# A four-layer graph network on one core: quarter sums, plane splits and merged additions change engines, and the planner's durations change

## The chip, the cores and the metric

The kernel runs on one core of a Trainium2 chip. The metric is the device time of one launch in microseconds (us), lower is better. A core has five engines with queues of their own: TensorE (PE, with its weight loads as PEld), VectorE (DVE), ScalarE (ACT), GpSimd (POOL) and SyncE (SP), which here only issues DMAs. Each queue runs in the order in which it was written. TensorE writes into eight banks of PSUM (512 fp32 values per partition each), and VectorE and ScalarE bring the results from there to SBUF.

## What is computed

The input is 128 graphs of 64 nodes with 512 features, and one 64 x 64 adjacency matrix for all. Four layers follow each other, all in fp32:

```python
h = relu(layernorm(x))
x = x + attention0(h)          # q, k, v with bias, 8 heads of 64, masked softmax
h = relu(layernorm(x))
x = x + attention1(h) @ Wo + bo
h = relu(layernorm(x))
x = x + normalised((h Wq)(h Wk)^T * adj) @ (h Wv)      # no softmax, rows divided by their norm
h = relu(layernorm(x))
o = attention3(h) @ w_proj + b_proj
x = x + o + layernorm(o) * gamma + beta
```

## The kernel before

**Tiling.** The 8192 rows are cut into 16 blocks of 512 rows, eight graphs each. The main loop runs over n = 0 to 63, 16 blocks for each of the four layers. In layers 0, 1 and 3 an iteration does the projections q, k and v of its block, the scores, and the values product of the block before; layers 1 and 3 add an output projection o, one or two iterations later. Layer 2 has two projections (`a2`, in which two weights are folded into one, and `v2`).

**Projections.** A projection is a 512 x 512 x 512 product. It is not done with eight block products of 256 but with seven, in the manner of Strassen and Winograd: sums of blocks of the input (`S`, or `SO` for the output projection; made by `sums_x`), sums of blocks of the weights (made once per weight), and additions of the seven products into the four blocks of the result. A part of the seven is split again in the same way into products of 128: the table `LEVEL2` says which, "423" for most. For such parts `sums_q` makes four more sums of 128 columns from the input's blocks, and the products of 128 are added in quarters. In `projection`, the string `parts` is "423" or "43", products "a", "b" and "c" are those whose quarters go to several blocks, and `add(dst, ps)` adds a PSUM bank to the result on VectorE. For the first product of a block `copy` or `copy_4` brings the bank over on ScalarE (with the bias of q and k), and products that are needed twice go to the small tiles `p5`, from which GpSimd adds them.

**Layer norm and transposes.** For a block, VectorE takes mean and variance, GpSimd the inverse root, ScalarE normalises (`xin`). The projections want the block with features on the partitions. `turn` does this by DMA: the fp32 values are split into two planes of 16 bits (tile `z`, 1024 elements of uint16), a DMA transposes them (`hp`), and ScalarE weaves them together into `hT`. The splitting copy is an argument with the default `dve.tensor_copy`; for the softmax weights the call hands over `act.copy`.

**Which engine makes the sums.** `sums_x` takes an engine for the block sums, and for the quarter sums of each part it chooses VectorE if the part is in `ON_DVE` (which is "2"), else GpSimd:

```python
        for q in parts:
            on = dve if q in ON_DVE else gps
            x[q] = sums_q(x[int(q)], room, (eng if eng is dve else on).tensor_tensor, fine and q != "3")
```

**The order of the work.** The code does not issue instructions. It records them in a `Plan`, which orders them and then issues all in `issue`, for which reason every instruction stands under one line of the profile, L285 (in the changed kernel this line has the number 291). `Plan.order` is a list scheduler: each step has a busy time and a lateness from `duration`, it becomes ready when its inputs are, and of the ready steps the planner takes the one that can start first, and of equals that with the lowest rank. The rank is the time at which the work must be done for TensorE to run in the recorded order, plus an offset per kind of step from the table `PREFER`. Steps that read PSUM get `HASTE` taken off the rank. The planner also gives out the eight banks. A block of PSUM is opened by its first product and its bank is free when its last reader is done. `PORT` is a lateness that also marks VectorE instructions with two inputs in SBUF, which the planner lets exclude GpSimd. Thus a new duration or offset can move any instruction on any queue, DMA issues included.

**Names in the profile.** `mm` is any of the PSUM banks; `w` any weights; `kT`, `qT`, `v` results of projections (`kT` also holds the result of o in layer 3); `oT` the attention's output, `SO` its sums; `s` the scores; `xo` the block to which the layer's result is added; `p` the tiles `p5`.

Of the kernel before, what the change touches and what calls it, by code (L numbers as in the profile page):

```python
# [56 lines left out]
class Plan:  # L57
# [106 lines left out]
    def order(self):  # L164
# [56 lines left out]
        opened, first = set(), 0  # L221
        self.start, self.bank = {}, {}
        while len(self.start) < n:
            best = None
            idle = sorted(t for b, t in enumerate(freed) if b not in holds)
            for e in engines:
                pick = None
                for i in here[e]:
                    at = max(ready[i], free[e])
# [34 lines left out]
            for h in uses[i]:  # L264
                last[h] = max(last.get(h, 0.0), at + busy + (0.0 if e == "tensor" else late))
                left[h] -= 1
                if not left[h]:
                    del holds[self.bank[h]]
                    freed[self.bank[h]] = last[h]
            for u, lag in users[i]:  # L270
                same = self.steps[u][0] == e
                ready[u] = max(ready[u], at + busy - lag + (0.0 if same and not moves else late))
                wait[u] -= 1
                if not wait[u]:
                    here[self.steps[u][0]].append(u)
# [35 lines left out]
class Pool:  # L311
# [28 lines left out]
PORT = 150.5  # L340
# [5 lines left out]
ON_DVE = "2"  # L346
WINDOW = 6
RESERVE = 0
HASTE = 0.0
PREFER = {  # L350
    "gps dma_start out_0_dram<-xo 2048": -12683,
    "gps dma_start x1<-kT": -7145,
    "gps dma_start x1<-row": -3460,
    "gps dma_start x1<-xo": -18648,
    "gps memset mhalf<- 8": 4917,
    "gps memset ones<- 1": -3867,
    "gps tensor_scalar ve<-mv 1": 622,
    "gps tensor_scalar ve<-mv 4": -1287,
    "gps tensor_tensor S2<-S 128": 9247,
    "gps tensor_tensor S2<-S2 128": -37406,  # L360
    "gps tensor_tensor S<-S 512": -89087,
    "gps tensor_tensor S<-hT 512": -1496,
    "gps tensor_tensor SO2<-SO 128": 12636,
    "gps tensor_tensor SO2<-SO2 128": 10398,
    "gps tensor_tensor SO<-oT 512": 2203,
    "gps tensor_tensor hT<-hT 128": 1226,
    "gps tensor_tensor kT<-kT 128": 5636,
    "gps tensor_tensor kT<-kT 256": 3369,
    "gps tensor_tensor kT<-kT 512": -42897,
    "gps tensor_tensor oT<-oT 128": 2476,  # L370
    "gps tensor_tensor qT<-qT 128": -134,
    "gps tensor_tensor qT<-qT 256": -1241,
    "gps tensor_tensor rn<-ss 8": -17140,
    "gps tensor_tensor row<-hT 128": -1603,
    "gps tensor_tensor row<-row 128": 8443,
    "gps tensor_tensor rs<-ve 1": 12875,
    "gps tensor_tensor s<-hT 128": -26189,
    "gps tensor_tensor s<-s 1024": -13182,
    "gps tensor_tensor s<-s 128": -40765,
    "gps tensor_tensor v<-v 128": -615,  # L380
    "gps tensor_tensor w<-w 128": -892,
    "gps tensor_tensor w<-w 512": 3785,
    "gps tensor_tensor xo<-xo 128": 44131,
    "gps tensor_tensor xo<-xo 512": -445,
    "sca activation kT<-mm 128": -119261,
    "sca activation kT<-mm 256": -39612,
    "sca activation qT<-mm 128": -41982,
    "sca activation qT<-mm 256": -11513,
    "sca activation s<-s 1024": 49040,
    "sca activation s<-s 256": 11077,  # L390
    "sca activation xin<-xin 512": 38622,
    "sca copy hT<-hp 1024": 66109,
    "sca copy hT<-mm 512": 10088,
    "sca copy kT<-mm 128": -16208,
    "sca copy kT<-mm 512": -19133,
    "sca copy oT<-mm 512": -12905,
    "sca copy p5<-mm 128": 237,
    "sca copy qT<-mm 128": 625,
    "sca copy qT<-mm 256": 54924,
    "sca copy qT<-mm 512": 3166,  # L400
    "sca copy s<-hp 1024": 447,
    "sca copy s<-mm 512": 10472,
    "sca copy v<-mm 128": 7235,
    "sca copy v<-mm 256": -3409,
    "sca copy v<-mm 512": -11450,
    "sca copy w<-mm 128": -19703,
    "sca copy w<-mm 256": -8441,
    "sca copy xo<-mm 128": 3488,
    "sca copy xo<-mm 256": -4935,
    "sca copy z<-mm 512": 4852,  # L410
    "sca copy z<-s 1024": 11870,
    "syn dma_start SO<-in_L2_gnn_Wk_dram": -11583,
    "syn dma_start a2d<-z": 2446,
    "syn dma_start adj2<-in_adj_dram": 31047,
    "syn dma_start bk0<-in_L0_gnn_bk_dram": 17099,
    "syn dma_start bk1<-in_L1_gnn_bk_dram": 6479,
    "syn dma_start bq0<-in_L0_gnn_bq_dram": -9211,
    "syn dma_start bq1<-in_L1_gnn_bq_dram": 6149,
    "syn dma_start bv1<-in_L1_gnn_bv_dram": 5734,
    "syn dma_start hp<-z": -502,  # L420
    "syn dma_start oT<-in_L2_gnn_Wq_dram": 4334,
    "syn dma_start oT<-in_L2_gnn_Wv_dram": 17636,
    "syn dma_start out_0_dram<-qT": 14773,
    "syn dma_start out_0_dram<-xo": 16686,
    "syn dma_start row<-in_L0_gnn_bv_dram": -25453,
    "syn dma_start row<-in_L3_gnn_ln_beta_dram": -11958,
    "syn dma_start row<-in_L3_gnn_ln_gamma_dram": -3573,
    "syn dma_start w<-a2d": -3983,
    "syn dma_start w<-in_L0_gnn_Wk_dram": 15922,
# [85 lines left out]
def duration(eng, op, aps, a, k):  # L515
# [3 lines left out]
    if eng == "tensor":  # L519
        kdim, m = aps[1].partition_size(), aps[1].free_size()  # L520
        if op == "transpose":
            return 109, 200
# [1026 lines left out]
```

## Time and profile before

| | us |
|---|---|
| median of three runs | 2807.11 (2804.61 to 2808.24) |
| the profiled run, its own time | 2805.3 |
| its span, first to last instruction | 2803.5 |
| mean granted TensorE clock | 0.999 |

The profiled run is 1.8 us under the median. Instructions of one shape are grouped in one row, "x 250" times with busy time and the mean of one. The slices of the span show that TensorE's clock was granted in full throughout, and that TensorE is at 90% or more in all slices but the last:

```profile
PE   9999999999999999999999999999999999999998
PEld 8889888988898999999999898989899899898897
DVE  7877778877877777777777666666788998988998
ACT  5677677777665665666755454445555655565662
POOL 5667767668977767677679855556777887887885
PEclk9999999999999999999999999999999999999999
```

The layers lie at about 0 to 680, 680 to 1450, 1450 to 1970 and 1970 to 2803 us. VectorE is fullest in layer 3, from slice 29 on. The costliest TensorE group and some groups of the other engines:

```profile
L285 PE MATMUL mm<-S,w 128*128 128x256 f32 (+1 forms) x4600 | 907.0, 338 | 9.2 <-ACT kT L285 6.2
L285 ACT COPY hT<-hp 128x1024 uint16<-128x1024 uint16 x252 | 331.0, 1354 | 17.3 <-DMA hp<-z 15.1
L285 POOL TENSOR_TENSOR s<-s,mx 128x1024 f32<-128x1024 f32 x96 | 186.8, 1947 | 109.4 <-DVE mx L285 87.0
```

A row gives line, engine, operation, tiles and shape, then count, busy time in us, mean of one in ns, and the time for which the engine stood idle just before these instructions with what ended it. An idle engine that is not the bottleneck costs nothing.

### The profile page before, as it was taken

Reading aid. Unit: us, or ns where it says so; the run is one execution under the profiler, and the core shown is the slowest. Engines: PE = TensorE matmul, PEld = TensorE weight load, DVE = VectorE, ACT = ScalarE, POOL = GpSimd, SP = SyncE. Lnnn points to the kernel's source line nnn. Section 1 sums busy time; section 2 is a strip of 40 time slices with the busy share of each in tenths; the row PEclk is TensorE's granted clock in tenths of the full one; section 3 lists DMA queues with packets and bytes.
Section 4 is the critical chain, followed back from the end, with each engine's and each line's share of the span. In section 5 each row is a group of like instructions: output and inputs, shape, how many; then the busy total and the mean of one; then the engine's idle time right before and its main releaser. Section 6 shows DMA issues by size and latency. Waiting matters only on the chain. (4 is left out here: it accounts for less than half of the span.)

```text
span 2803.5 us, 72722 instructions
## 1 busy us (share of the span) xinstructions
PE 2758.9 (98%) x29259; PEld 2506.2 (89%) x29259; DVE 2185.6 (78%) x4436; ACT 1691.6 (60%) x2885; POOL 1999.4 (71%) x2381
## 2 busy tenths in 40 slices
PE   9999999999999999999999999999999999999998
PEld 8889888988898999999999898989899899898897
DVE  7877778877877777777777666666788998988998
ACT  5677677777665665666755454445555655565662
POOL 5667767668977767677679855556777887887885
PEclk9999999999999999999999999999999999999999
DMA  5765566666466455464566675656545655655655
GB/s 140 155 144 132 145 145 147 150 135 143 95 116 119 91 117 97 94 133 88 100 150 128 158 180 147 166 135 163 110 76 92 114 99 92 116 97 91 116 86 113
DMA packets 635026, 344.54 MB, mean 123 GB/s; under 512 B 484288, under 2 KB 565952, under 8 KB 634688
## 3 DMA queue, kind: packets, MB, share of 16 engines
q1 hardware_dynamic: 601424, 273.83, 42.8%
q0 software_dynamic: 33264, 66.06, 14.7%
q8 instruction: 230, 3.77, 0.5%
q14 instruction: 108, 0.88, 0.1%
HBM read 120.63 MB, written 102.76 MB: 80 GB/s over the span
## 5 line engine op out<-in xcount | busy, mean ns | idle before, releaser
L285 PE MATMUL mm<-S,w 128*128 128x256 f32 (+1 forms) x4600 | 907.0, 338 | 9.2 <-ACT kT L285 6.2
L285 PEld LDWEIGHTS mm<-S,w 128*128 128x128 f32 x4600 | 732.0, 191 | 74.7 <-ACT kT L285 9.6
L285 PE MATMUL mm<-hT,w 128*128 128x128 f32 (+1 forms) x3392 | 605.2, 310 | 5.9 <-ACT kT L285 2.0
L285 PEld LDWEIGHTS mm<-hT,w 128*128 128x128 f32 x3392 | 520.5, 191 | 51.7 <-ACT p L285 2.7
L285 PE MATMUL mm<-w,S 128*128 128x256 f32 (+1 forms) x2604 | 520.4, 339 | 0.8 <-ACT v L285 0.7
L285 PEld LDWEIGHTS mm<-w,S 128*128 128x128 f32 x2604 | 419.0, 191 | 37.5 <-issue 1.0
L285 DVE TENSOR_TENSOR qT<-mm,qT 128x128 f32<-128x128 f32 (+2 forms) x578 | 264.4, 485 | 173.4 <-PE mm L285 82.6
L285 PE MATMUL mm<-w,hT 128*128 128x128 f32 (+1 forms) x1872 | 343.1, 315 | 6.2 <-DVE v L285 4.4
L285 DVE TENSOR_TENSOR kT<-mm,kT 128x512 f32<-128x512 f32 (+2 forms) x616 | 274.4, 471 | 91.3 <-ACT kT L285 68.1
L285 ACT COPY v<-mm 128x128 f32<-128x128 f32 (+1 forms) x380 | 169.4, 447 | 291.7 <-PE mm L285 262.9
L285 ACT COPY hT<-hp 128x1024 uint16<-128x1024 uint16 x252 | 331.0, 1354 | 17.3 <-DMA hp<-z 15.1
L285 PEld LDWEIGHTS mm<-w,hT 128*128 128x128 f32 x1872 | 287.1, 191 | 31.0 <-issue 3.6
L285 DVE TENSOR_TENSOR v<-mm,v 128x512 f32<-128x512 f32 (+2 forms) x578 | 261.1, 480 | 61.9 <-PE mm L285 25.8
L285 PE MATMUL mm<-w,SO 128*128 128x256 f32 x1302 | 262.0, 336 | 5.2 <-DVE kT L285 5.0
L285 POOL TENSOR_TENSOR s<-s,mx 128x1024 f32<-128x1024 f32 x96 | 186.8, 1947 | 109.4 <-DVE mx L285 87.0
L285 ACT ACTIVATE xin<-xin,nb,rs 128x512 f32<-128x512 f32 x256 | 198.8, 814 | 98.5 <-DVE nb L285 98.5
L285 ACT COPY s<-hp 128x1024 uint16<-128x1024 uint16 x188 | 246.2, 1353 | 0.0
L285 POOL TENSOR_TENSOR qT<-qT,p 128x256 f32<-128x256 f32 (+1 forms) x170 | 110.0, 659 | 185.4 <-DVE qT L285 105.5
L285 PEld LDWEIGHTS mm<-w,SO 128*128 128x128 f32 x1302 | 213.6, 191 | 28.5 <-DVE kT L285 10.4
L285 DVE COPY z<-xin 128x1024 uint16<-128x1024 uint16 x252 | 197.8, 801 | 30.3 <-ACT xin L285 29.6
L285 ACT COPY z<-s 128x1024 uint16<-128x1024 uint16 x188 | 191.6, 1049 | 26.4 <-POOL s L285 26.2
L285 POOL TENSOR_TENSOR v<-v,p 128x256 f32<-128x256 f32 (+1 forms) x170 | 124.3, 742 | 96.4 <-DVE v L285 86.1
(120 smaller groups left out, 4685.9 us busy)
## 6 DMA issues: line engine op xcount, KB each, us to landing
xin<-x SPq DMA_DIRECT2D x128, 256.0 KB, 4.7
xin<-in_x_dram SPq DMA_DIRECT2D x64, 256.0 KB, 3.9
x<-row POOLq DMA_DIRECT2D x16, 1024.0 KB, 16.9
xin<-out_dram SPq DMA_DIRECT2D x64, 256.0 KB, 3.9
out_dram<-row POOLq DMA_DIRECT2D x16, 1024.0 KB, 9.3
x<-xo POOLq DMA_DIRECT2D x15, 1024.0 KB, 12.3
out_dram<-xo POOLq DMA_DIRECT2D x15, 1024.0 KB, 9.3
xo<-in_x_dram SPq DMA_DIRECT2D x32, 256.0 KB, 3.9
```

The source lines that it names most:

```text
L285: getattr(getattr(self.nc, eng), op)(*a, **k)
```

## The change

Five things are done together.

1. `ON_DVE` becomes empty: the quarter sums of part "2" go from VectorE to GpSimd.
2. `turn` splits planes with `act.copy` by default: the 256 splits of normalised blocks and of one weight go from VectorE to ScalarE.
3. Where a projection has parts "2" and "3", their quarters are added to both result blocks by one VectorE instruction with twice the columns. For this `projection` gets the whole result tile and views its first two blocks as `top`.
4. The planner treats a bank as usable by one engine at a time: a step that uses a bank starts only after the other engines' earlier steps at it. A new `LOAD` of 110 ns stands before TensorE's use of anything from another engine.
5. `duration` is refined: separate values for ScalarE's forms and small operations, latenesses of 160 to 220 instead of 150 to 200, `PORT` 160.5 instead of 150.5, the extra time of the joined group in `relate` 580 instead of 300. `HASTE` is 1674 instead of 0, and nearly all of the some 200 offsets in `PREFER` have new values.

```diff
@@ Plan.order
+        used = [{} for _ in range(self.banks.taken)]
...
-                    at = max(ready[i], free[e])
+                    at = max([ready[i], free[e], *(
+                        t + (LOAD if e == "tensor" else 0.0) for h in uses[i] for x, t in used[h].items() if x != e
+                    )])
...
             for h in uses[i]:
-                last[h] = max(last.get(h, 0.0), at + busy + (0.0 if e == "tensor" else late))
+                if e != "tensor":
+                    used[h][e] = at + busy + late
+                last[h] = max(last.get(h, 0.0), at + busy + (0.0 if e == "tensor" else late + LOAD))
...
                 same = self.steps[u][0] == e
-                ready[u] = max(ready[u], at + busy - lag + (0.0 if same and not moves else late))
+                load = LOAD if self.steps[u][0] == "tensor" else 0.0
+                ready[u] = max(ready[u], at + busy - lag + (0.0 if same and not moves else late + load))
@@ constants
-PORT = 150.5
+PORT = 160.5
+LOAD = 110
...
-ON_DVE = "2"
+ON_DVE = ""
...
-HASTE = 0.0
+HASTE = 1674.0
@@ duration (some of it)
-            return 109, 200
-        pass_ = max(n * 0.842, 111 if m > HD else HD * 0.842)
+            return 109, 220
+        pass_ = max(n * 0.8438, 111.8 if m > HD else HD * 0.842)
...
-        fixed = {"scalar_tensor_tensor": 140, "tensor_reduce": 100}.get(op, 85)
+        fixed = {"scalar_tensor_tensor": 125, "tensor_reduce": 100}.get(op, 68)
...
-        own = isinstance(k.get("scale"), bass.AP)
-        return max(240 + 0.49 * n, (1.32 if out.dtype == U16 else 1.4 if own else 0.95) * n), 170
+        if out.dtype == U16:
+            return (947 if out.ap[-1][0] == 1 else 1211), 200
+        if psum:
+            return (55 + 0.836 * n, 180) if op == "copy" else (175 + 0.711 * n, 180)
+        return (717 if isinstance(k.get("scale"), bass.AP) else 105 + 0.834 * n), 180
@@ turn
-    def turn(dst, src, nm, split=dve.tensor_copy):
+    def turn(dst, src, nm, split=act.copy):
@@ projection
+        if prod is prod_N:
+            top = t[:, 0:2, :].rearrange("p u (j v) -> p j u v", j=2)
+        else:
+            top = t[:, :, :H2].rearrange("p (j u) v -> p j u v", j=2)
...
-            if i in ("a", "b", "c"):
-                for q in parts[1:]:
-                    s, at = int(q), pv[:, pre[q]]
-                    if i == "c":
-                        add(pair(s, c21), twice(at))
-                    else:
-                        add(quad(s, 0 if i == "a" else c12), at)
+            if i in ("a", "b", "c") and parts[1:]:
+                if parts[1:] == "23":
+                    Q, at = top, pv[:, 2:4]
+                else:
+                    s = int(parts[1:])
+                    Q, at = Y[s].unsqueeze(1), pv[:, pre[parts[1:]]].unsqueeze(1)
+                if i == "c":
+                    q = Q[:, :, :, P:] if c21 == 1 else Q[:, :, 1, :].rearrange("p j (v e) -> p j v e", v=2)
+                    add(q, at.unsqueeze(2).to_broadcast([P, len(parts) - 1, 2, P]))
+                else:
+                    s = 0 if i == "a" else c12
+                    add(Q[:, :, s // 2, s % 2 * P : s % 2 * P + P], at)
@@ relate
-        plan.end(300)
+        plan.end(580)
```

The calls of `projection` hand over the tile instead of a region of it. Nothing of the mathematics changes but the place and the grouping of these additions.

## The prediction

> **What bounds the kernel now.** I read the page's busy times first. They say that TensorE carries the span:
>
> ```profile
> PE 2758.9 (98%) x29259; PEld 2506.2 (89%) x29259; DVE 2185.6 (78%) x4436; ACT 1691.6 (60%) x2885; POOL 1999.4 (71%) x2381
> ```
>
> The 98% is too kind: a matmul's end is modelled, so short waits between two matmuls pass as busy. In the timeline, eight passes of 128x256 start every 1.73 us (0.216 each), six of 128x128 every 0.67 us (0.112), and a group of 128 passes of 64x64 takes 2.03 us. With two passes per matmul and the program's counts that is 3544 x 0.432 + 4062 x 0.223 + 256 us of small, transposing and 512-wide matmuls = **2692 us** of matmul work. The profiled run took 2805.3 us (span 2803.5). Of the 113 us between, about 11 lie before the first projection product, about 9 after the last matmul, and 39.3 are the waits "issue" of the next view, most of them 0.3 us at a change of tile size. The rest is what a better order could win.
>
> The waits of the weight loads (engine and tile that waited, released by; total, times, longest) name that rest:
>
> ```profile
> PEld mm L285 <- issue: 39.3, 110, 1.6
> PEld mm L285 <- DVE kT L285: 17.4, 42, 0.9
> PEld mm L285 <- ACT kT L285: 12.2, 16, 2.2
> PEld mm L285 <- DVE v L285: 5.1, 7, 1.6
> PEld mm L285 <- ACT p L285: 4.3, 5, 1.2
> ```
>
> All named waits together are 57 us: about 28 on VectorE, 23 on ScalarE, 6 on GpSimd and others. By windows, layer 0 (0 to 700 us) has 18, layer 1 seven, layer 2 (1400 to 2050) five, layer 3 (2050 to 2804) 18. So the prize is 57 us at most, and no engine but TensorE is near its limit in the mean. **Where** it is lost shows in layer 3. Its score groups follow each other by 52.25 us in the timeline; those of layer 1, with the same products per iteration, by 50.94. VectorE is busy 47.2 of 52 us there (windows view), 38.6 of 51 in layer 1. The chain of waits of one such iteration:
>
> ```profile
> 2133.73 0.20 DVE oT L285
> 2133.93 2.99 DVE SO L285
> 2136.92 0.33 DVE v L285
> 2137.25 0.61 DVE kT L285
> 2137.86 0.04 issue
> 2137.90 4.18 PE mm L285 x22
> ```
>
> Two quarter sums of 128 columns (one pass of the helper `sums_q` for part "2") hold VectorE for 3 us. Behind them in its queue stand the additions out of PSUM, and the weight load at 2137.90 waits for one of these. The next view (durations min/median/max) shows that this is not arithmetic:
>
> ```profile
> L285 POOL TENSOR_TENSOR SO<-SO x62: 443/462/910, 753.8 to 2752.9; 128x128 f32<-128x128 f32 x62
> L285 DVE TENSOR_TENSOR SO<-oT x31: 279/541/3147, 766.5 to 2751.1; 128x128 f32<-128x128 f32 x31
> ```
>
> 279 ns when free, 3147 at worst, while a GpSimd instruction runs. GpSimd's own spread is far smaller.
>
> **The change, part by part.** Matmul counts by shape are equal before and after (3544, 4062 and the rest), so the 2692 us stay. The prices come from these rows:
>
> ```profile
> L285 DVE COPY z<-xin 128x1024 uint16<-128x1024 uint16 x252 | 197.8, 801 | 30.3 <-ACT xin L285 29.6 <-DMA a2d<-z 0.2
> L285 DVE TENSOR_TENSOR kT<-mm,kT 128x128 f32<-128x128 f32 x244 | 62.4, 281 | 50.4 <-ACT kT L285 43.1 <-PE mm L285 6.7 <-ACT p L285 0.4
> L285 ACT COPY z<-s 128x1024 uint16<-128x1024 uint16 x188 | 191.6, 1049 | 26.4 <-POOL s L285 26.2
> ```
>
> 1. *Quarter sums of part "2" to GpSimd* (`ON_DVE` empty). 308 instructions leave VectorE: rows hT 55.5, S 47.1 + 21.3, SO 50.7 + 21.3, oT 38.5 = 234 us. On GpSimd the same shapes cost 0.46 to 0.57 us: 152 us. Here a rule speaks against it: the Trainium skill, "GPSIMD Engine Reference", section "Engine selection", puts elementwise adds on VectorE, since two-input operations are about twice as slow on GpSimd. By the rule the move frees 308 x 0.28 = 86 us and costs 172. By the trace it frees 234 and costs 152. The rule's GpSimd price holds; its VectorE price does not where GpSimd is busy 71% of the time, and I take the trace.
> 2. *Plane splits to ScalarE* (`turn`). 256 copies leave VectorE (197.8 + 4.8 = 203 us) and land on ScalarE at the price of the same copy out of `s`, 1.049 us: 268 us. Bounds: 0.80 (VectorE's price) and 1.35 (ScalarE's interleaving copy `hT<-hp`); the equal shape and direction decide. The skill's "Trace Analysis", section "Optimizing Scalar/DVE Operations", says that VectorE is the faster where it has a performance mode, and that moving pays once it is saturated. The rows agree with the first half: 65 us more engine time by this move. At 91% in layer 3 the second half applies there, but in layer 0, VectorE 79%, it does not, so there this part alone is a loss of cover.
> 3. *Quarters of products 2 and 3 in one addition.* 676 additions of 128 columns go (172 us by the rows' busy times), 169 of 512 columns come (0.66 us, 112 us), those of 256 stay 338. VectorE minus 60 us. The wait is not new: both were read from one bank after the same product, which was free only after both.
> 4. *The planner*: one engine at a bank, 110 ns for a weight load, longer and separate durations, 1674 ns of haste for readers of PSUM. It issues nothing, but all queues are reordered, the weights' and inputs' DMAs on SP too (same 1179 in number). Before, VectorE and ScalarE wait for one another at a shared bank (VectorE `p` for ScalarE `kT` 24.2 us, ScalarE `p` for VectorE `qT` 15.7) in a plan that did not count it. In the changed program's TensorE order, the matmul work between two products on one bank, in which a reader must fit, is 0.5 to 1.1 us in 19 places before and 15 after; in layer 0 it is 11 before and none after. A reader needs about 1 us there (0.58 of copy and some 0.2 at each side). Twelve of the new 15 are in layer 3, behind the values groups, 1.04 us: about 0.2 us each, 3 us.
>
> New loads: VectorE 2186 - 234 - 203 - 60 = **1690 us (60%)**, ScalarE **1960 (70%)**, GpSimd **2150 (77%)**. In layer 3 per iteration: VectorE 47.2 - 6.2 - 3.2 - 1.4 = 36, GpSimd 40.9 + 4 = 45 of 52 (86%), ScalarE 30 + 4 = 34. In layer 0 ScalarE goes from 71% to 81%.
>
> **Sum.** Layer 3: 52.25 - 50.94 = 1.31 us for 15 iterations = 20 us; VectorE there falls below what layer 1 runs with at no loss, so I take 17, less 3 for the narrow places = 14. Layer 0: 18, of which 4 are the start; I take 8 of 14 for the wider places, as ScalarE, now fuller, causes most of them. Layer 1: 3 of 7; layer 2: 2 of 5. Minus 2 for copies of 1.05 us in front of bank readers. Gain **25 us**: 2805 - 25 = 2780. The runs' median is 1.8 us above the profiled run, so I say **2781 us**.
>
> **Rivals.**
> - *Nearly all goes* (10%): the plan now matches the chip in every layer. 57 less 4 at the start less 5 = 48 us: 2758. For: layer 1 shows iterations with no loss at all. Against: GpSimd and ScalarE are fuller.
> - *Half of it is given back, at ScalarE in layer 0* (16%): ScalarE's 23 us of waits stay or grow, only layer 3's 14 are won, 3 are lost again: 2794. The edge of this case is no change.
> - *Slower, GpSimd late for the output projections* (18%): after a values group it needs four sums of 1.28 and now twelve quarter sums instead of eight, 5.1 + 6.1 = 11 us, between its softmax work of 1.9 us each. In the new order TensorE reaches the first quarter product 18.6 us after the values in layer 1 (median; 26.9 before), 22.6 in layer 3 (26.0), at least 8.2 (21.3). Should GpSimd's queue bring the sums 1.5 us too late in each of the 31 iterations, 46 us are lost against 25 won: 2828. It decides from 0.8 us on. Against: GpSimd is free 22% of layer 1's time even after the change, and its sums stood in no wait of note before (6 us in all).
> - *It does not do what it says*: excluded by the counts, 308 to GpSimd, 256 to ScalarE, 676 for 169.
>
> The forecast itself has 56%, with an own range of 2768 to 2793. A measurement of this kernel tells 0.2% (5.6 us) from no change. Faster by more is the forecast, the first rival and half of the second: 0.74; within 0.2% 0.08; slower 0.18. The range 2755 to 2812 leaves some of the first rival and most of the slower one out.
>
> **What would show it.** Right: named waits of the weight loads near 30 us, those on VectorE `kT` below 5; layer 3's score groups 51.3 us apart or less; no VectorE instruction on `SO` in the chain; busy VectorE 1690, ScalarE 1960, GpSimd 2150. Wrong: weight loads waiting for GpSimd `SO`, `oT` or `S` by more than 15 us (slower rival), or for ScalarE `kT`, `qT` and `p` by more than in the 16 us they had in layers 0 and 1 (second rival). Unknown is the head: the first weights are issued in another order, worth up to 2 us either way.

## The result: 2.9% slower, and the profile after

| | before | after |
|---|---|---|
| median of the runs, us | 2807.57 | 2888.03 (2881.85 to 2894.4, four runs) |
| ratio, 95% interval | | 1.0289 (1.0262 to 1.0316) |
| profiled run, its own time; span | 2805.3; 2803.5 | 2881.85; 2880.1 |
| mean granted TensorE clock | 0.999 | 0.987 |

The forecast of 2781 us, a gain of 1%, is wrong in sign, and the time lies 76 us above its range. The changed kernel's busy times, and TensorE's row of its 40 slices of 72 us:

```profile
PE 2773.3 (96%) x29259; PEld 2515.4 (87%) x29259; DVE 1796.0 (62%) x3365; ACT 1902.3 (66%) x3141; POOL 2064.4 (72%) x2689
...
PE   9999999999899899898899999999999999999998
```

VectorE lost 390 us of work, as intended, and no engine but TensorE is near its limit. But TensorE's row now has eights in slices 11 to 20, which are layer 1. To say how much each layer loses I take the starts of successive score groups in the trace and subtract the matmul work that lies between them, at the unit times of the prediction. What TensorE loses in this way, in us (worked out from the traces; how large layer 2's loss is depends on the unit times of its small matmuls, the differences between kernels do not):

| | layer 0 | layer 1 | layer 2 | layer 3 | head, tail, 0 to 1 |
|---|---|---|---|---|---|
| before | 25.8 | 14.4 | 20.6 | 30.9 | 9.2 |
| after | 11.5 | **93.6** | 30.8 | 30.4 | 10.4 |

Layer 0 gained 14 us, layer 3 nothing, layer 2 lost 10 and layer 1 lost 79. The waits of the weight loads (engine and tile that waited, released by; total, times, longest) of the whole changed kernel:

```profile
PEld mm L291 <- ACT kT L291: 70.2, 34, 13.1
PEld mm L291 <- issue: 40.2, 103, 1.6
PEld mm L291 <- ACT v L291: 14.2, 27, 1.1
PEld mm L291 <- POOL rs L291: 10.7, 13, 0.9
PEld mm L291 <- DVE v L291: 9.8, 13, 1.7
...
PEld mm L291 <- DVE kT L291: 2.8, 9, 0.3
```

VectorE `kT` fell from 17.4 to 2.8 us, as forecast. ScalarE `kT` rose from 12.2 to 70.2. The same view for layer 1 alone (700 to 1480 us) says that this is not many small waits but seven long ones, and ScalarE's own waits there say what it stood at:

```profile
PEld mm L291 <- ACT kT L291: 62.3, 7, 13.1
```

```profile
ACT hT L291 <- DMA hp<-z: 68.6, 7, 13.3
```

Before, the second of these lines was 7.5 us in six waits:

```profile
ACT hT L285 <- DMA hp<-z: 7.5, 6, 3.0
```

So ScalarE was not too full: it stood still seven times, about 10 us each, at the copy that weaves a transposed block together, because the transpose had not landed. The `kT` copies, from which TensorE's banks come free, stood behind it in ScalarE's queue. The chain of waits over one of these places (start, duration, what):

```profile
1163.36 0.70 ACT xin L291
1164.06 0.93 ACT z L291
1164.99 0.03 ACT kT L291
1165.02 18.40 DMA hp<-z
1183.41 0.02 issue
1183.44 0.02 ACT hT L291
1183.46 1.18 issue
1184.64 0.25 ACT p L291
1184.88 0.28 ACT kT L291
1185.16 0.04 issue
1185.21 4.80 PE mm L291 x19
```

A transpose issued at 1165.02 took 18.40 us. The rows of all 444 transposes, after and then before (SyncE's time for issuing one, in ns: min/median/max; below it us from issue to landing):

```profile
L291 SPq DMA_TRANSPOSE hp<-z x444: 1231/1277/10451, 35.7 to 2797.9; - x148
...
DMA to landing us min/median/max: 3.0/3.3/18.5
```

```profile
L285 SPq DMA_TRANSPOSE hp<-z x444: 1231/1263/2612, 34.5 to 2725.7; - x148
...
DMA to landing us min/median/max: 3.0/3.2/15.2
```

The medians are alike. New are the slow ones: of the transposes whose landing is recorded (some 390 of the 444), 34 take over 8 us after and two before. What lay ahead of this one is in GpSimd's timeline:

```profile
1163.61 1.39 POOL L291 DMA_DIRECT2D x<-xo  x1 [0.17 <-POOL qT L291]
1166.08 1.42 POOL L291 TENSOR_TENSOR qT<-qT,p 128x256 f32<-128x256 f32 x2 [1.08 <-ACT qT L291]
1167.44 1.28 POOL L291 DMA_DIRECT2D x<-row  x1
```

These are the two DMAs by which GpSimd adds layer 1's result to `x1` in memory, 1 MB each; the view of DMA issues gives them a median of 10.6 and 15.5 us to land. Here the transpose went out 1.4 us behind the first and 2.4 us ahead of the second. The first landed at 1176.4, the transpose at 1183.4 and the second at 1186.2. Before, in all blocks of layer 1 after 850 us, the pair stood 0.7 to 2.4 us **behind** the last transpose of a group, and the next transpose came 28 to 30 us later. After, in both phases of the order the next transpose comes 0.8 to 1.7 us behind a DMA of the pair.

One more thing has to be explained: in every second block the late transposes cost nothing. The planner does know that SyncE's DMAs are late behind GpSimd's (`moved`, `added` in `order`): it expects 19 us there and gives the readers that slack. In the other blocks it placed one transpose 0.3 us **ahead** of `x1<-xo` and expected it to land as if nothing stood ahead of it. On the chip ScalarE's split for that transpose came a little later than planned, GpSimd's DMA did not wait for it, and the order of the two was turned round. That reading, "theory A", is what the experiments test.

### The profile page after: what moved, and what is told of

Same layout as the page of the kernel before. It is cut to its first block, busy times and chain, and to the rows that moved or that the text cites. A ratio compares the mean times of both kernels' runs of the same rounds, so it can differ in the third digit from the quotient of the medians.

```text
span 2880.1 us, 72001 instructions
## 1 busy us (share of the span) xinstructions
PE 2773.3 (96%) x29259; PEld 2515.4 (87%) x29259; DVE 1796.0 (62%) x3365; ACT 1902.3 (66%) x3141; POOL 2064.4 (72%) x2689
## 3 DMA queue, kind: packets, MB, share of 16 engines
q8 instruction: 229, 3.75, 0.5%
## 4 chain that ended last, share of the span: by engine, by line
PE 57%; POOL 15%; DVE 9%; issue 7%; DMA 6%; ACT 4%; SPq 1%; POOLq 0%; DVEq 0%; ACTq 0%
PE mm L291 57%; DMA hp<-z 4%; POOL SO L291 3%; DVE st L291 3%; POOL s L291 2%; POOL S L291 2%; POOL kT L291 2%; DVE kT L291 2%; POOL w L291 1%; ACT xin L291 1%; DVE qT L291 1%; ACT z L291 1%; DMA xin<-x 1%; SPq L291 1%; POOL qT L291 1%
## 5 line engine op out<-in xcount | busy, mean ns | idle before, releaser
L291 PE MATMUL mm<-S,w 128*128 128x256 f32 (+1 forms) x4600 | 926.7, 340 | 2.3 <-DVE qT L291 1.4
L291 PEld LDWEIGHTS mm<-S,w 128*128 128x128 f32 x4600 | 747.5, 193 | 65.8 <-ACT kT L291 2.0
L291 PE MATMUL mm<-w,S 128*128 128x128 f32 (+1 forms) x2604 | 529.6, 339 | 4.7 <-ACT v L291 2.3
L291 DVE TENSOR_TENSOR kT<-mm,kT 128x256 f32<-128x256 f32 (+1 forms) x433 | 261.4, 613 | 366.4 <-PE mm L291 177.2
L291 DVE TENSOR_TENSOR v<-mm,v 128x256 f32<-128x256 f32 (+2 forms) x440 | 254.2, 587 | 178.3 <-POOL v L291 87.5
L291 DVE TENSOR_TENSOR qT<-mm,qT 128x512 f32<-128x512 f32 (+1 forms) x440 | 254.5, 590 | 154.7 <-PE mm L291 103.1
L291 ACT COPY z<-xin 128x1024 uint16<-128x1024 uint16 x252 | 259.3, 1069 | 3.0 <-DMA a2d<-z 2.5
L291 POOL TENSOR_TENSOR S<-hT 128x512 f32<-128x512 f32 (+1 forms) x172 | 194.2, 1129 | 87.6 <-PE mm L291 60.5
L291 PE MATMUL mm<-w,SO 128*128 128x128 f32 (+1 forms) x1302 | 253.5, 335 | 0.0
L291 POOL TENSOR_TENSOR SO<-oT 128x512 f32<-128x512 f32 (+1 forms) x93 | 93.0, 1000 | 178.0 <-ACT oT L291 115.2
## 6 DMA issues: line engine op xcount, KB each, us to landing
x<-row POOLq DMA_DIRECT2D x16, 1024.0 KB, 15.5
x<-xo POOLq DMA_DIRECT2D x15, 1024.0 KB, 10.6
```

The costliest lines, as they stand in the source:

```text
L291: getattr(getattr(self.nc, eng), op)(*a, **k)
```

## The experiments

Fourteen kernels were run, in four lots, each beside the kernel before. "Same order" means that the plan is made as it was, and that only the named instructions change place or engine as they are issued.

**1. Hold back seven DMAs.** In the changed kernel, `x1<-xo` is issued next to its partner `x1<-row`, two GpSimd instructions later, where the plan had them further apart than in the other blocks.

```diff
+    def held(self, order):
+        out = list(order)
+        for i in order:
+            if self.kind(i) != "gps dma_start x1<-xo":
+                continue
+            j = out.index(i)
+            n = next((m for m in range(j + 1, len(out)) if self.kind(out[m]) == "gps dma_start x1<-row"), None)
+            if n is None or self.start[out[n]] - self.start[i] > 12000:
+                continue
...
+            out.insert(n, i)
+            del out[j]
...
-        for i in self.order():
+        for i in self.held(self.order()):
```

> The changed kernel with every queue as it is, but for seven DMAs of layer 1 on GpSimd's queue (block added into x, every second block), which stand two instructions later, just ahead of the next accumulating DMA. Theory A (collision: a transpose that is issued just behind an accumulating DMA lands after 18 us instead of 3, ScalarE's queue stands still behind it and TensorE behind ScalarE): the seven waits of TensorE in layer 1 of 5 to 13 us, 62 us together, go; 2888 becomes about 2825. Theory B (ScalarE is simply too full with the splits, the late landing is only where it shows): the waits stay or move, 2870 to 2890.

Measured: 2823.35 us, ratio 1.0045 (1.003 to 1.006). Seven instructions of 72,000, moved by one or two places, are worth 65 us. Layer 1 loses 34.6 instead of 93.6, the other layers are as in the changed kernel. Of the seven long waits in layer 1 six are gone; 8.9 us in one place at 780 us stay. ScalarE `kT` among the waits of the weight loads:

```profile
PEld mm L305 <- ACT kT L305: 15.6, 27, 8.9
```

Transposes of up to 11.2 us at issue remain in this trace, but behind the pair, where the plan has slack for them. Theory A holds for the bulk of the loss.

**2. and 3. The splits alone, in both orders.** The 252 splits of normalised blocks go back to VectorE in the changed kernel's order, and over to ScalarE in the order of before.

```diff
@@ changed kernel, splits on VectorE
             eng, calls = self.steps[i][:2]
+            if eng == "scalar" and self.kind(i) in ['sca copy z<-xin 1024']:
+                eng, calls = "vector", [("tensor_copy" or op, a, k) for op, a, k in calls]
@@ kernel before, splits on ScalarE
+            if eng == "vector" and self.kind(i) in ['vec tensor_copy z<-xin 1024']:
+                eng, calls = "scalar", [("copy" or op, a, k) for op, a, k in calls]
```

> The changed kernel with the order of all steps kept, but the 252 splits of normalised blocks issued on VectorE, at their place in that order. Theory A: the splits are done earlier than in ScalarE's queue, so that the transposes are issued ahead of the accumulating DMA as planned, and 40 to 60 us of the 81 come back: 2825 to 2850. Theory B (too much work on ScalarE) says the same or a bit more: 2815 to 2840. If neither holds and the order itself is bad, 2870 or more.

> The kernel before with its order kept, but the 252 splits issued on ScalarE. Theory A (the splits do harm only where an accumulating DMA stands close; before, the next transpose is 28 us behind one): slower by 5 to 25 us, 2812 to 2832, from ScalarE being late for PSUM in an order that was not made for it, and no transposes of 18 us in layer 1. Theory B: 30 us or more, 2840 and up.

Measured: 2901.08 us (1.0339, 1.0319 to 1.0358) and 2934.32 us (1.0449, 1.0427 to 1.0471). Both expectations of theory A were missed. In the order of before the same splits on ScalarE cost 126 us: every layer loses (54.3, 52.6, 65.4 and 48.4 us), ScalarE `qT` becomes the largest named wait of the weight loads (37.7 us). In the changed order the splits on VectorE cost 13 us more than on ScalarE, layer 1 still losing 73.2. In both orders the splits cost less on the engine for which their places were found.

**4. The quarter sums alone, in the order of before.**

```diff
+            if eng == "vector" and self.kind(i) in ['vec tensor_tensor S2<-hT 128', 'vec tensor_tensor hT<-hT 128', 'vec tensor_tensor SO2<-oT 128', 'vec tensor_tensor oT<-oT 128', 'vec tensor_tensor SO<-oT 128', 'vec tensor_tensor S<-hT 128']:
+                eng, calls = "gpsimd", [(None or op, a, k) for op, a, k in calls]
```

> The kernel before with its order kept, but the 308 quarter sums of part 2 issued on GpSimd. If VectorE's waits[...] were what layer 3 lost (as the prediction said), its iterations go from 52.25 to about 51 us: 2785 to 2795. If GpSimd becomes the late one instead, no gain or a loss: 2805 to 2830.

Measured: 2821.02 us (1.0047, 1.0032 to 1.0062), a loss of 13 us. In layer 3 (2050 to 2750 us) VectorE's busy time fell from 632 to 557 us of 700, yet the period rose from 52.25 to 52.75 us; layer 1 lost some 8 us too. VectorE waited more instead. Its wait for the small products that GpSimd adds went from 9.0 us to

```profile
DVE v L287 <- POOL v L287: 66.8, 41, 6.3
```

Its waits for ScalarE's `kT`, at `kT` and `p`, grew as well, from 92 to 167 us together. Which of the two lengthened the period is not shown. The 3 us quarter sums that the prediction saw on VectorE were real, but taking them away gave layer 3 no time.

**5. Hold back every such DMA.** In the changed kernel each layer-1 accumulating DMA with a planned transpose less than 6 us behind it goes behind that transpose.

```diff
+            late = [t for t in turns if 0 < self.start[t] - self.start[i] < 6000]
+            if not late:
+                continue
+            end = self.start[late[-1]] + 1400
+            j = out.index(i)
+            n = next(m for m in range(j + 1, len(out)) if self.start[out[m]] > end or i in self.steps[out[m]][2])
...
+            out.insert(n, i)
+            del out[j]
```

> The changed kernel with its order kept, but every accumulating DMA of layer 1 that has a transpose planned within 6 us behind it stands behind those transposes on GpSimd's queue. Theory A: no transpose of layer 1 takes over 5 us to land any more, and the 20 us that layer 1 still loses above the kernel before in the run with seven DMAs held go as well: 2823 becomes 2800 to 2812. If the late DMAs hold up GpSimd's own queue or the reading of x instead: 2820 or more.

Measured: 2817.87 us (1.0039, 1.0025 to 1.0054). "No slow transposes" was missed: a DMA's place in GpSimd's queue says only what GpSimd does before it, and SyncE was often later still, so 8.8 to 10.9 us at issue remained. Layer 1 loses 34.9, as in experiment 1. Of that, 13 lie in one place at 780 us, to which experiment 13 comes back.

**6. and 7. Quarter sums back on VectorE, and the merged additions in two halves,** both in the order of experiment 1.

```diff
@@ 6: sums_x and issue
+            if q == "2":
+                plan.second |= set(range(first, len(plan.steps)))
...
+            if i in self.second:
+                eng = "vector"
@@ 7: projection and issue
+                if parts[1:] == "23":
+                    plan.merged.add(len(plan.steps))
...
+            if eng == "vector" and i in self.merged:
+                halves = []
+                for op, x, k in calls:
+                    for j in range(2):
+                        halves.append((op, [v[:, j] if isinstance(v, bass.AP) else v for v in x], k))
+                calls = halves
```

> The changed kernel with the seven DMAs held (2823) and, at the same places in the order, the 308 quarter sums of part 2 back on VectorE. Theory C: in layers 2 and 3 it is GpSimd, filled by these sums, that is late with the additions of the tiles p, for which VectorE waits with its own additions (waits of VectorE for GpSimd at v, kT and qT: 21 us before, 171 in the changed kernel) and TensorE for VectorE. Then these waits fall below 80 us and layer 3's score groups come nearer than 52.5 us: 2800 to 2818. Theory D (VectorE's waits[...] are as bad): same or slower, 2820 to 2840.

> The changed kernel with the seven DMAs held (2823), but each merged addition of quarters issued as two of half its size at the same place: 169 additions of 512 columns and 169 of 256 more. VectorE gets about 60 us more work. If the merging was worth something on the path: 2828 to 2840; if it was free: 2821 to 2826; a gain would mean that the bank's first half is wanted earlier.

Measured: 2829.47 us (1.0082, 1.0067 to 1.0097) and 2827.45 us (1.0071, 1.0056 to 1.0086), against 2823.35. So in the order made for it, GpSimd's share of the sums is worth 6 us between the medians (layer 3: 37.7 us lost with them on VectorE, 30.2 on GpSimd), the reverse of experiment 4. Theory C was missed: VectorE's waits for GpSimd at `v`, `kT` and `qT` fell only from 174 to 125 us, and the time rose while they fell, so these waits alone do not decide layer 3's time. The merging of additions is worth some 4 us between the medians; the intervals of the two ratios overlap.

**8. The planner alone.** The kernel before with the new rule for banks, `LOAD` and the new durations; engines, additions, offsets and `HASTE` 0 as before.

```diff
-PORT = 150.5
+PORT = 160.5
+LOAD = 110
-        plan.end(300)
+        plan.end(580)
@@ and Plan.order and duration as in the change
```

> The kernel before with its own engines, additions and offsets, but with the new planner rule (one engine at a bank, a weight load of 110 ns) and the new durations. The offsets were not made for these, so the order is another one; it has four transposes 6 to 12 us behind an accumulating DMA in every second block of layer 1, none nearer. If the truer model alone makes a better order: below 2800. If offsets and model only work together: 2820 to 2880.

Measured: 2837.29 us (1.0115, 1.0095 to 1.0135). Layer 1 loses 14.6 as before, but layer 3 55.7, ScalarE `kT` 39.5 us. The old offsets belong to the old model: here new durations and a new rule, with offsets found for others, gave a worse order.

**9. Splits on VectorE and DMAs held back.** Experiments 1 and 2 together.

```diff
+        for i in self.held(self.order()):
+            if eng == "scalar" and self.kind(i) in ["sca copy z<-xin 1024"]:
+                eng, calls = "vector", [("tensor_copy", a, k) for op, a, k in calls]
```

> The changed kernel with the layer-1 accumulating DMAs held back as before (2823 us so far), and the 252 splits issued on VectorE at their old places. With the splits on VectorE but no holding the time was 2901. Theory A (collisions cost layer 1 its time whichever engine splits): layer 1 falls from 73 to about 35 us, 2901 - 40 = 2860 (2845 to 2875), and the rest over 2823 is the price of splits that stand in VectorE's queue at places chosen for ScalarE (layers 0, 2 and 3: 16 + 5 + 12). Theory E (in this order the splits on VectorE cost layer 1 as much as the collisions do): 2885 or more.

Measured: 2864.33 us (1.0203, 1.019 to 1.0217). Layer 1 falls from 73.2 to 35.6 us, the same as with the splits on ScalarE; what is left over 2823 lies in layer 0 (28.4 instead of 11.7), the passage to layer 1 (9.2 instead of 1.0) and layer 3 (42.5 instead of 30.2). So experiment 2 failed theory A only because two things were added there: the collisions cost layer 1 some 38 us with the splits on VectorE (59 on ScalarE, experiment 1), and in this order the splits are worth 41 us on ScalarE.

**10. A collision made in the order of before.** The kernel before, with the second DMA of each pair issued some 28 us later, just ahead of a transpose.

```diff
+            if self.kind(i) != "gps dma_start x1<-row":
+                continue
+            t = next((t for t in turns if self.start[t] > self.start[i]), None)
...
+            n = next(m for m in range(j + 1, len(out)) if self.start[out[m]] > self.start[t] - 1000 or i in self.steps[out[m]][2])
...
+            out.insert(n, i)
+            del out[j]
```

> The kernel before with its own order, engines and additions; only GpSimd's second accumulating DMA of each layer-1 block (the one of the row sums) is issued about 28 us later, just ahead of a GpSimd addition planned 0.7 us before the next transpose. Theory A (a transpose issued 1 to 2 us behind an accumulating DMA lands after 18 instead of 3.3 us, and that alone makes TensorE wait): the transposes behind the moved DMAs take 8 to 11 us to issue, ScalarE's wait for them goes from 15 to over 100 us in all, layer 1's loss from 14 to 60 or more and the time to 2850 to 2900. Theory F (the collision hurts only where splits are on ScalarE): transposes are late but the time stays below 2820. If the moved DMAs go out behind the transposes, nothing is told and the time is 2805 to 2815.

Measured: 2849.29 us (1.0147, 1.0131 to 1.0162). The number is at the edge of what theory A gave, but for another reason. The transposes' row in the middle of layer 1 (850 to 1400 us):

```profile
L302 SPq DMA_TRANSPOSE hp<-z x80: 1231/1278/4661, 865.4 to 1372.8; - x80
...
DMA to landing us min/median/max: 3.1/4.4/10.6
```

A single DMA made the transposes 1.8 and 5.4 us behind it 3.3 to 4.7 us at issue, not 8 to 11, and in this stretch ScalarE waited 2.9 us for transposes in all. The 3.3 us that each block lost are at another line:

```profile
PEld mm L302 <- ACT xo L302: 36.5, 24, 2.1
```

By the timeline of one block, GpSimd's 1.3 us for issuing the moved DMA fall into its densest stretch, a VectorE sum beside it takes 3.75 us (the same sum 0.23 before), and the additions behind that are late: between 850 and 1400 us ScalarE's waits for VectorE's additions to `xo` grew from 14.6 to 34.4 us. The experiment is no proof that a collision alone is enough; it says that one 1 MB DMA is not what two are.

**11. and 12. The change in layer 0 alone, and in layers 0 and 3.** All that the change does to engines, additions, rule, durations, haste and offsets is done for the instructions of the layers in `NEW` only, which is `{0, 3}` in the second kernel.

```diff
+            rank[i] += (PREFER if self.age[i] else OLD).get(self.kind(i), 0.0)
...
+                        t + (LOAD if e == "tensor" else 0.0) for h in uses[i] for x, t in used[h].items() if x != e and self.age[i]
...
+            on = dve if q == "2" and plan.now not in NEW else gps
...
+            split = act.copy if plan.now in NEW else dve.tensor_copy
...
+NEW = {0}
```

> The whole change (engines, merged additions, planner rule, durations, haste, offsets) for the instructions of layer 0 alone; those of layers 1 to 3 with the engines, additions, rule, durations and offsets of before. In the plan layers 1 to 3 have the period of before and few transposes behind an accumulating DMA. If layer 0's gain (25.8 to 11.5 us of loss) is its own: 2808 - 14 = 2794 (2788 to 2800), below both kernels. If it is bought at the cost of layer 1: 2805 or more.

> The whole change for layers 0 and 3 alone, layers 1 and 2 as before. Theory A: layer 3, which lost 30 us with and without the change, gains nothing, so within 6 us of the version with layer 0 alone: 2790 to 2802, against 2781 had the prediction been right about layer 3 (14 us more won).

Measured: **2794.68 us (0.9957, 0.9944 to 0.9969)** and 2800.26 us (0.9977, 0.9968 to 0.9986). Layer 0's gain is its own: 11.9 us lost there instead of 25.8, and layers 2 and 3 as before. Layer 3's share of the change is no gain but a loss of 5.6 us between the two medians (32.0 us of loss in layer 3 against 28.5). In layer 1 one block alone loses 12.3 us, the one at 780 us again:

```profile
PEld mm L292 <- ACT kT L292: 9.6, 1, 9.6
```

In its plan the first DMA of the pair stands 0.4 us behind the third of four transposes; in its trace it goes out 2.7 us ahead of it, and the fourth takes 8.35 us at issue.

**13. That pair held back too,** in the version of experiment 11.

```diff
+        j = kinds.index("gps dma_start x1<-xo")
+        k = kinds.index("gps dma_start x1<-row", j)
+        n = kinds.index("gps tensor_tensor SO<-oT 512", k) + 1
+        return out[:j] + out[j + 1 : k] + out[k + 1 : n] + [out[j], out[k]] + out[n:]
```

> The version with the change in layer 0 alone (2795 us), with one more edit: the first pair of accumulating DMAs of layer 1 (planned at 764.3 and 765.5 us, 0.4 us behind the third of four transposes but on the chip 2.7 us ahead of it) is issued behind GpSimd's next sum of 512 columns, so behind all four transposes. Theory A (the 12 us that the second block of layer 1 still loses, in this version as in the changed kernel with held DMAs, are one more such collision): ScalarE's 9.8 us wait for a transpose goes and the time is 2784 (2780 to 2788). Theory G (that block is late because work of layer 0 runs into it, and the transpose is only the last to be seen): 2790 to 2796.

Measured: **2788.51 us (0.994, 0.9927 to 0.9954)**, the fastest of all that do the whole work, 0.6% below the kernel before. ScalarE's wait for the transpose in that stretch goes from 9.8 to 0.4 us, the weight loads' wait for ScalarE `kT` there from 9.6 to 0.8, and that block loses 1.6 instead of 12.3 us. It is the same collision. Each of its five runs is faster than each of the five of experiment 11. The gain is 6 us and not 11, since the next block, into which the two DMAs moved, loses 4.2 instead of 0.6.

**14. None of these DMAs.** The changed kernel's order, with layer 1's accumulating DMAs not issued; its result lacks these sums, so it is no candidate.

```diff
+            if eng == "gpsimd" and self.kind(i) in ["gps dma_start x1<-xo", "gps dma_start x1<-row"]:
+                continue
```

> The changed kernel with all instructions in its own order, but the accumulating DMAs of layer 1 are not issued, so that the sums of that layer's output and of its row terms are missing from the result. Theory A (these DMAs in front of transposes are the whole loss of layer 1): layer 1 loses 15 to 25 instead of 94 us, ScalarE waits for no transpose over 2 us, and the time is 2888 - 75 = 2813 (2805 to 2820), still no less than before, since layer 3 and layer 2 lose what they lost. Theory G (something else in layer 1 is late as well): above 2825.

Measured: 2786.45 us (0.9931, 0.9918 to 0.9945), 27 us less than expected. Layer 1 loses 7.8 us instead of 93.6 and layer 2, whose first transposes stand behind the last of these DMAs, 23.8 instead of 30.8. The sum that was expected had kept losses of experiment 1, in which six blocks of layer 1 still lose 1.5 to 2.3 us each and two lose 6.9 and 11.9; here every block loses 0.4 to 0.7. Two things go with them here, and this run does not part them: the rest of the collisions, and GpSimd's 2.7 us per block for issuing the pair, which experiment 10 showed not to be free. ScalarE waits for no transpose over 2.4 us, and none takes over 2.8 us at issue:

```profile
ACT hT L293 <- DMA hp<-z: 10.9, 10, 2.4
```

```profile
L293 SPq DMA_TRANSPOSE hp<-z x444: 1231/1273/2831, 35.8 to 2705.3; - x148
```

## Why the prediction was wrong

**The step that failed** is the fourth part of the change: "It issues nothing, but all queues are reordered, the weights' and inputs' DMAs on SP too (same 1179 in number)". Having said that all queues are reordered, it put a price only on the space between two products on one bank, 3 us, and counted SyncE's DMAs instead of asking what each now stands behind. GpSimd's 63 DMAs were not looked at. In the changed order GpSimd's layer-1 DMAs cost about 86 us in layer 1 and 7 in layer 2 (changed kernel against experiment 14, GpSimd's issuing time included). In the order of before they can't have cost layer 1 more than the 14.4 us that it lost in all. Of the difference, 65 us came back when seven of them were moved by a place or two (experiment 1). Before's own trace had the two signs: a longest landing of 15.2 us among transposes of 3.2, of a transpose that went out 0.7 us behind such a pair at 836 us, and accumulating DMAs which from then on in layer 1 all stood just behind a group of transposes.

**What bounds the kernel** was right: TensorE's work of 2692 us is the same, and layer 0's waits were in reach. **Layer 0** was to gain 8 us and gained 14, as it did alone (experiment 11). Its prize was misread: the whole view of the named waits from 0 to 700 us adds up to 26 us, and the prediction's 18 are the six largest of them (its four layers add up to 48 us, and not to the 57 that it gives for all).

**Layer 3** was to gain 14 us, because VectorE's load there falls below what layer 1 runs with. VectorE's busy time between 2050 and 2750 us did fall, from 632 to 510 of 700, but the loss went from 30.9 to 30.4, and the score groups are 52.6 us apart (median) where at most 51.3 were forecast. The step from "VectorE is 91% busy and stands in the chain" to "its relief is TensorE's gain" is what failed: experiment 4 relieved VectorE alone and the layer lost 8 us; experiment 12 added layer 3 to the change in layer 0 and the time rose by 5.6. The waits changed their name. The weight loads that waited by over 0.1 us for another engine within one period of 52.7 us, after and then before (in brackets how long, and released by which engine):

```profile
2209.12 0.52 PEld L291 LDWEIGHTS mm<-w,hT 128*128 128x128 f32 x4 [0.60 <-ACT v L291]
...
2232.48 0.52 PEld L291 LDWEIGHTS mm<-hT,w 128*128 128x128 f32 x4 [0.88 <-POOL rs L291]
```

```profile
2218.11 1.59 PEld L285 LDWEIGHTS mm<-S,w 128*128 128x128 f32 x8 [0.48 <-ACT kT L285]
...
2221.59 0.30 PEld L285 LDWEIGHTS mm<-hT,w 128*128 128x128 f32 x2 [0.16 <-DVE kT L285]
...
2242.41 1.59 PEld L285 LDWEIGHTS mm<-w,SO 128*128 128x128 f32 x8 [0.78 <-DVE kT L285]
```

1.42 us by VectorE and ScalarE became 1.48 by ScalarE and GpSimd. Which offset of the plan keeps them there was not tried, so why layer 3 gained nothing stays open. So do some 3 of layer 2's 10 us, which experiment 14 did not bring back.

**The prices of the parts** were worked out engine by engine, and that is not what decided. VectorE fell to 1796 us and not to 1690, ScalarE came to 1902 (1960 forecast), GpSimd to 2064 (2150). VectorE's miss is one of counting: the durations of all its instructions, added up, fell from 2435 to 1937 us, as much as forecast (234 + 203 + 60), but they overlap in part, and busy time counts an overlap once. No run shows that one of the three misses cost time. The splits were priced at 65 us more engine time, with the hint that alone in layer 0 they would be a loss of cover; experiment 3 shows 126 us of loss in an order not made for them, experiment 9 41 us of gain in one that is. The Trainium skill's rule ("Perfetto Trace Analysis", "Optimizing Scalar/DVE Operations") that an offload may make sense once VectorE is saturated (a weaker word than the "pays" of the prediction) decided neither. The quarter sums likewise: 13 us lost in the one order, 6 won in the other. The same section warns that moving work between GpSimd and VectorE might not help, since they share a port; the prediction did not weigh that sentence. The outcome of experiment 4 agrees with it; that the port is the reason, no run here shows. The trace's 0.46 to 0.57 us on GpSimd was the right price, but the sum of 234 us freed and 152 spent had no bearing on the time.

**The rivals.** "GpSimd late for the output projections" had the right sign and the wrong place: the weight loads' waits for `SO`, `oT` and `S` stay small in the changed kernel, and its sign of failure, 15 us of such waits, did not come. "Half given back at ScalarE in layer 0" named ScalarE `kT` as the sign, and it came, 70 us, but in layer 1 and not because ScalarE was full. No rival had a DMA in it.

## What to carry to other kernels

Where a change reorders queues, look at every pair of queues that share the DMA engines, and at what each latency-critical transfer now stands behind: one number per transfer, the distance to the large DMA ahead of it, would have pointed to this. Where a plan puts a short transfer a few tenths of a us ahead of a long one on another queue, the chip need not keep that order (here 0.3 us ahead in the plan became 1.4 us behind on the chip); either keep a distance that the plan's own errors can't cross, or place the long one behind. And an engine change is not worth "time freed minus time spent": the same 252 copies were worth minus 126 or plus 41 us, by the order in which they were put.

## What the runs showed of the hardware

A DMA transpose issued close to a pair of accumulating DMAs of 1 MB each from GpSimd lands late: in the chain above, between the two, after 18.4 us instead of 3.3; at 889.4 us, 0.8 us behind both, after 15.8 us, within 0.2 us of the second's landing. SyncE itself is held for up to 10.5 us at issuing the next one. Behind one such DMA it is 3.3 to 4.7 us at issue and at most 10.6 to landing (experiment 10). The Trainium skill ("DMA: Bandwidth & Descriptors", "Issuing engines are not separate DMA queues") says that DMAs of all issuing engines run on the same 16 DMA engines and interleave. The trace agrees, and its packets show what the interleaving costs. The DMA view counts them by queue (q0 is GpSimd's, q1 SyncE's; packets, MB, time taken as a share of the 16 engines). From 894 to 901 us of the changed kernel, where transposes wait beside a pair, and from 1174 to 1176 us of the kernel before, where they run alone:

```profile
q0 software_dynamic: 617, 1.23, 94.9%
q1 hardware_dynamic: 599, 0.15, 17.1%
```

```profile
q1 hardware_dynamic: 1566, 0.39, 101.8%
```

The two queues get through about as many packets, but GpSimd's are of some 2 KB and the transposes' of some 250 bytes. So SyncE's queue moves 21 KB per us beside the pair and 195 alone, and the 262 KB of one transpose (128 x 1024 values of 16 bits) take 12 us instead of 1.3, an estimate from these rows. In the chain above, between 1169 and 1179 us, it is 777 packets of GpSimd's against 814 of SyncE's. By these counts the delay is for the most part a sharing of turns, in which small packets lose. What the trace doesn't explain is that there no packet of SyncE's queue moves in the first 4 us after 1165, while GpSimd's do.

A stall also costs TensorE's clock. Around the stall of the chain above, the windows of the trace (stretch, its length, busy time and count of PE, PEld, DVE, ACT and POOL, the granted clock, DMA share, GB/s):

```profile
1160.00:1168.00 8.00, 8.00 (x51) 7.40 (x50) 3.75 (x7) 8.00 (x17) 3.77 (x5) 1.00 0.53 59
1168.00:1185.00 17.00, 4.22 (x143) 3.80 (x141) 3.14 (x6) 3.74 (x7) 3.24 (x3) 0.70 1.22 140
1185.00:1190.00 5.00, 4.79 (x21) 4.39 (x22) 0.62 (x2) 0.81 (x3) 0.00 (x0) 0.65 1.12 275
1190.00:1195.00 5.00, 5.00 (x36) 4.69 (x35) 3.33 (x5) 1.93 (x6) 3.79 (x5) 1.00 0.01 4
```

After 13 us without work the granted clock is 0.65 in the mean of the next 5 us and then 1.00 again. In narrower windows it is 0.50 from 1174.8 to 1188.5 us, that is from 2.6 us after the last matmul before the stall until 3.3 us into the work behind it, and 1.00 from 1188.5. So the stall costs some 1.7 us more than its length (an estimate: 3.3 us at half the clock, or 5 x 0.35). The Trainium skill ("TensorE: Matmul & The Clock Gate", part 1) has the clock at half after about 3.4 us of idleness; the half agrees, the wait was 2.6 us here. Such stalls are where the mean clock of 0.987 comes from; it is 0.997 in experiment 1 and 0.999 in experiment 14, with the same matmuls.
